# All engines in the order of the program: background pieces, their evictions and small shares of vector and scalar work in a two-layer graph network

## The chip, the cores and the metric

The kernel runs on one core of a Trainium2 chip. Its time is the device time of one execution in microseconds (us). The engines are named as in the profile: PE is TensorE (PEld its weight loads), DVE is VectorE, ACT is ScalarE, POOL is GpSimd, SP is SyncE, which issues DMAs. PEclk is the clock that TensorE was granted, as a share of full speed. All data are 32-bit floats.

## The reference

Two residual layers over 16 graphs of 1024 nodes with 256 channels. The first weighs the adjacency matrix by how similar the nodes' channel means are, makes queries from it, and runs attention with four heads of 64. The second multiplies by a normalised adjacency, and has two linear maps, each with a batch norm over all 16 × 1024 rows.

```python
# layer 0; x is (16, 1024, 256)
h = jnp.maximum(_layernorm(x, axis=-1), 0.0)
fea = jnp.transpose(h, (0, 2, 1))
c_adj = jnp.mean(fea, axis=1)
diff = c_adj[:, None, :] - c_adj[:, :, None]
A = jnp.abs(jnp.abs(jax.nn.sigmoid(diff) - 0.5) - 0.5) * 2.0
A_s = (A + jnp.transpose(A, (0, 2, 1))) * 0.5
g = jax.nn.relu(jnp.einsum('bcn,bnm->bcm', fea, adj[None] * A_s) * para.reshape(1, C, N))
q = jnp.transpose(g, (0, 2, 1)).reshape(B, N, 4, 64).transpose(0, 2, 1, 3)
kv = (h @ kv_w).reshape(B, N, 2, 4, 64).transpose(2, 0, 3, 1, 4)
attn = jax.nn.softmax(jnp.einsum('bhnd,bhmd->bhnm', q, kv[0]) * scale, axis=-1)
x = x + jnp.einsum('bhnm,bhmd->bhnd', attn, kv[1]).transpose(0, 2, 1, 3).reshape(B, N, C)
# layer 1
h = jnp.maximum(_layernorm(x, axis=-1), 0.0)
A_norm = adj + jnp.eye(n)
deg = A_norm.sum(0) + A_norm.sum(1) - jnp.diagonal(A_norm)
A_hat = A_norm * rsqrt(deg)[:, None] * rsqrt(deg)[None, :]
agg = jnp.einsum('nm,bmd->bnd', A_hat, h).reshape(-1, d)
y = jax.nn.relu(_batchnorm(agg @ W1.T + b1, g1, be1))
x = x + _batchnorm(y @ W2.T + b2, g2, be2).reshape(b, n, -1)
```

## The kernel before

**Two parts.** `layers(False)` does the first layer and the second one up to the hidden values `y` (512 channels), which go to HBM (`y1_d`), as does x after the first layer (`x1_d`). The batch norm needs statistics over all graphs, so `second("f", flag)` starts when the last `y` is there: it loads `y` in 32 blocks, applies the norm and a relu on ACT (L707), multiplies by `w2` on PE (L717), and after a second batch norm (L738) transposes, adds x and stores the result (L750 to L757). This last stretch is called the tail. A `layers(True)` behind a condition does attention with a shift by the row maximum; it is not executed here.

**The attention loop** (`attention`, L583) sets the order. A graph has four units `(b, k, f)`: a pair of heads `k` and half of the nodes `f`. A unit has four steps, so a graph has 16 steps. On PE a step issues:

1. `scores` (L500): two score tiles, each then raised by an Exp on ACT (L508). Their PSUM pool has two buffers.
2. `finish` (L575), if a unit ended in the step before: four transposes of its output `os`, added to x on DVE (L579).
3. a TOP piece, if one is due: four transposes, either of broadcast channel means (`cbp`, L149) or of h (`htp`, L241).
4. `values` (L540): the product of the step before's Exp tiles with v.
5. `divide`, if that ended a unit: `sums` (L557), a product with ones of the accumulated Exp tiles `acc` (adds on DVE, L526 and L529). On DVE follow four reciprocals (L563), the product with `os` (L564), and two reductions that watch for overflow (L566, L567).
6. one to four background pieces from the generator `bg`.

**Background pieces.** `background(b)` yields, while graph b is in attention, the work of its neighbours in pieces of four or eight matmuls, each with an estimated cost in us (1.71): the queries of graph b+1 (`pg`, evicted by a multiply on DVE, L299, and a relu on ACT, L301), its keys and values (`pk`, L315 on ACT; `pv`, L332 on DVE), the aggregation of graph b-1 (`pa`, L368 on DVE), its hidden product (`py`, L386 on ACT, statistics on DVE, L387, store by POOL, L388), and the TOP pieces for graph b+2. As many pieces are issued in a step as `total`, spread over the 16 steps, makes due (L605). `weave` lets a side generator advance by one item with each piece.

Pieces share two PSUM banks:

```python
        def bank(name):
            return ps_mm.tile([P, FB], F32, tag="mm", name=name)
```

A piece that opens a bank waits until the second last user of the banks has been evicted.

**Vector and scalar work beside it.** `weights` (L247) makes the weighted adjacency of a query piece: a load of adj, two Abs (L261) and a Tanh (L268) on ACT, a product on DVE (L269), all in a pool of four buffers. `norm_relu` (L194) is a layer norm with relu: statistics on DVE (L211, L212), a reciprocal root on POOL (`rsqrt`, L76), relus on ACT (L218). `degrees` and `graph` (L161, L177) make the normalised adjacency once, in graph 0, in eight tiles that use the same four buffers as the adj tiles.

**What sets the order.** PE issues in the order of the program; DVE, ACT, POOL and SP are put in order by a scheduler:

```python
                with tc.manual_schedule(engines={mybir.EngineType.PE}):
                    run(norm_relu(0, True), differences(0), transposed(0))
                    weights(0, 2)
                    run(keys_values(0))
```

`second` stands outside of it, and all its engines are put in order by the scheduler.

Of the kernel before, what the change touches and what calls it, by code (L numbers as in the profile page):

```python
# [23 lines left out]
def gnn_two_layers_kernel(  # L24
# [38 lines left out]
    stats1 = const.tile([P, HC, B * NH, 6], F32, name="stats1")  # L63
    stats2 = const.tile([P, CC, B * NH, 6], F32, name="stats2")
# [16 lines left out]
    def layers(shifted):  # L81
# [20 lines left out]
        csums, cbcs, weighted = {}, {}, {}  # L102
        complete = set()

# [31 lines left out]
        nc.sync.dma_start(out=para_sb, in_=para.rearrange("(k p) n -> p k n", p=P))  # L136
# [3 lines left out]
        def broadcast_row(dst, col, name):  # L140

            for g in range(NT // 4):
                cb = p2.tile([P, 4, P], F32, tag="cb", name=f"cb_{name}_{g}")
                nc.vector.tensor_copy(
                    cb, col[:, 4 * g : 4 * g + 4].unsqueeze(2).to_broadcast([P, 4, P])
                )
                pt = bank(f"cbp_{name}_{g}")
                for j in range(4):
                    nc.tensor.transpose(pt[:, j * P : (j + 1) * P], cb[:, j, :], ident)  # L149
                nc.scalar.copy(dst[:, g * FB : (g + 1) * FB], pt)  # L150
                yield 0.5
# [9 lines left out]
        def degrees():  # L161
# [3 lines left out]
            for t in range(NT):  # L165
                a = load_adj_t(t, "at1")
                db = p2.tile([P, P], F32, tag="cb", name=f"db_{t}")
                nc.vector.tensor_mul(db, a[:, t * P : (t + 1) * P], ident)
                nc.vector.tensor_reduce(diag[:, t : t + 1], db, AX.X, ALU.add)
                nc.vector.tensor_reduce(col[:, t : t + 1], a, AX.X, ALU.add)  # L170
                yield 0.0
# [3 lines left out]
            yield 0.0  # L175

        def graph():  # L177

            dbc = p1.tile([P, N], F32, tag="cbc", name="dbc")
            yield from broadcast_row(dbc, dinv, "deg")  # L180
            for t in range(NT):
                a = load_adj_t(t, "at2")
# [11 lines left out]
        def norm_relu(b, first):  # L194


            tag = "a" if first else "b"
            src = xs[b]
            st6 = p2.tile([P, NT, 6], F32, tag="st6", name=f"st6_{tag}_{b}")
            mv = p2.tile([P, NT, 2], F32, tag="mv", name=f"mv_{tag}_{b}")  # L200
            sm = p2.tile([P, 3, NT], F32, tag="lnsm", name=f"lnsm_{tag}_{b}")
            if first:
                csums[b] = p2.tile([P, NT], F32, tag="csum", name=f"csum_{b}")
            h = p2.tile([P, NT, C], F32, tag="h", name=f"h_{tag}_{b}")
            hs[tag, b] = h
            for half in range(2):
                ts = range(half * NT // 2, (half + 1) * NT // 2)
                sl = slice(ts[0], ts[-1] + 1)
                rstd, shift, tmp = (sm[:, i, sl] for i in range(3))
                for t in ts:  # L210
                    nc.vector.bn_stats(st6[:, t, :], src[:, t, :])  # L211
                    nc.vector.bn_aggr(mv[:, t, :], st6[:, t, :])  # L212
                rsqrt(rstd, mv[:, sl, 1], EPS, tmp)
                nc.vector.scalar_tensor_tensor(
                    shift, mv[:, sl, 0], -1.0, rstd, op0=ALU.mult, op1=ALU.mult
                )
                for t in ts:
                    nc.scalar.activation(  # L218
                        h[:, t, :],
                        src[:, t, :],  # L220
                        AF.Relu,
                        bias=sm[:, 1, t : t + 1],
                        scale=sm[:, 0, t : t + 1],
                        accum_out=csums[b][:, t : t + 1] if first else None,
                    )
                yield 0.0

        TOP = -1.0

        def transposed(b):  # L230

            h = hs["a", b]
            hts[b] = []
            for k in range(CC):
                ht = p3.tile([P, N], F32, tag="ht", name=f"ht_{b}_{k}")
                hts[b].append(ht)
                for g in range(NH):
                    pt = bank(f"htp_{b}_{k}_{g}")
                    for j in range(FB // P):
                        t = g * (FB // P) + j  # L240
                        nc.tensor.transpose(  # L241
                            pt[:, j * P : (j + 1) * P], h[:, t, k * P : (k + 1) * P], ident
                        )
                    nc.vector.tensor_copy(ht[:, g * FB : (g + 1) * FB], pt)
                    yield 0.5

        def weights(b, upto):  # L247

            csum, cbc = csums[b], cbcs[b]
            made = weighted.setdefault(b, [])  # L250
            while len(made) <= min(upto, NH * NP - 1):

                q, th = divmod(len(made), NP)
                a = load_adj(q, th, f"adj_{b}_{q}_{th}")
                w = p4.tile([P, TH, FB], F32, tag="w", name=f"w_{b}_{q}_{th}")
                if b == 0:
                    nc.vector.tensor_reduce(
                        rows[:, q, th * TH : (th + 1) * TH], a, AX.X, ALU.add
                    )
                for t in range(TH):  # L260
                    nc.scalar.activation(  # L261
                        w[:, t, :],
                        cbc[:, q * FB : (q + 1) * FB],
                        AF.Abs,
                        bias=csum[:, th * TH + t : th * TH + t + 1],
                        scale=-1.0,
                    )
                nc.scalar.activation(w, w, AF.Tanh, scale=-0.5 / C)  # L268
                nc.vector.scalar_tensor_tensor(w, w, 1.0, a, op0=ALU.add, op1=ALU.mult)  # L269
                made.append(w)  # L270

        def differences(b):

            cbcs[b] = p1.tile([P, N], F32, tag="cbc", name=f"cbc_{b}")
            yield from broadcast_row(cbcs[b], csums[b], f"c{b}")

        def queries(b):
# [3 lines left out]
            for q in range(NH):  # L281
                cols = slice(q * FB, (q + 1) * FB)
                pgs = [bank(f"pg_{b}_{q}_{k}") for k in range(CC)]
                for th in range(NP):
                    i = q * NP + th
                    weights(b, i + 3)
                    for k in range(CC):
# [9 lines left out]
                        if th == NP - 1:  # L297
# [3 lines left out]
                            nc.scalar.activation(dst, dst, AF.Relu, scale=SCALE)  # L301
# [35 lines left out]
        def aggregate(b):  # L337

            h = hs["b", b]
# [8 lines left out]

            ats[b] = []
            for g in range(NH):  # L350
# [3 lines left out]
                for th in range(NP):  # L354
                    i = g * NP + th
                    load(i + 2)
# [14 lines left out]
        def hidden(b):  # L371
# [6 lines left out]
            for g, j in parts:  # L378
# [8 lines left out]
                nc.vector.bn_stats(stats1[:, j, i, :], y)  # L387
                nc.gpsimd.dma_start(out=y1_d[i][:, j, :], in_=y)  # L388
                yield 1.71

        def normed(b):
            halves = norm_relu(b, False)
            for half in range(2):
                while (b, half) not in complete:
                    yield 0.1
                yield from halves if half else [next(halves)]
            nc.gpsimd.dma_start(out=x1_d[b], in_=xs[b])

        def load_and_norm(b):
            load_x(b)  # L400
            yield 0.0
            yield from norm_relu(b, True)

        def weave(main, *sides):

            side = (piece for part in sides for piece in part)
            for cost in main:
                yield cost + next(side, 0.0)
            yield from side

        def background(b):

            nothing = iter(())
            more = b + 1 < B
            if b == 0:
                yield from weave(queries(1), degrees())
                yield from weave(keys_values(1), graph())
                yield from load_and_norm(2)
            else:
                if more:  # L420
                    yield from weave(queries(b + 1), normed(b - 1))
                    yield from keys_values(b + 1)
                else:
                    yield from normed(b - 1)
                yield from weave(
                    aggregate(b - 1), load_and_norm(b + 2) if b + 2 < B else nothing
                )
            products = hidden(b - 1) if b > 0 else nothing
            if b > 0:
                yield next(products)  # L430
            if b + 2 < B:

                made = chain(differences(b + 2), transposed(b + 2))
                for i in range(3):
                    yield TOP
                    yield next(made) + next(made)
                    if i == 0:
                        weights(b + 2, 2)
                    yield from islice(products, 3)
            yield from products  # L440

        def run(*parts):
            for part in parts:
                for _ in part:
                    pass
# [66 lines left out]
        class Unit:  # L512


            def __init__(self, b, k, f):
                self.at = (b, k, f)
                self.name = f"{b}_{k}_{f}"
                self.acc = None

# [31 lines left out]
            def divide(self):  # L551
# [8 lines left out]
                inv = p1.tile([P, FB], F32, tag="inv", name=f"inv_{self.name}")  # L560
                for j in range(FB // P):
                    c = slice(j * P, (j + 1) * P)
                    nc.vector.reciprocal(inv[:, c], self.pt[:, c])  # L563
                nc.vector.tensor_mul(self.os, self.os, inv)  # L564
# [252 lines left out]
```

## Time and profile before

| | us |
|---|---|
| median of 3 runs | 2894.21 |
| lowest, highest | 2893.5, 2896.43 |
| profiled execution, its own time | 2898.18 |
| its span in the trace | 2896.4 |
| PE busy in the span | 2733.5 (94%) |
| DVE busy | 1606.6 (55%) |
| ACT busy | 1257.2 (43%) |
| POOL busy | 189.6 (7%) |

The mean granted clock is 0.983. The span runs from the first recorded instruction to the last; the execution's own time is 1.8 us longer. Busy times are sums over the span; a matmul's end is modelled, so that records of one engine can overlap slightly. A line of a timeline has the start, the duration (of a run of like instructions), the engine, line and operation, the tile written and the tiles read, and in brackets the idle time before it and what ended it. In the list of waits a row has the engine, what waited, what it waited for, and then the sum in us, the number of times and the longest. Attention of graph 0 starts at 68.7 us in the trace, that of graph 1 at 199.8, and the neighbours after that about 158 us apart; the second part starts at 2590.3 and the tail at 2812.

### The profile page before, as it was taken

To read this page: it belongs to the slowest core of one execution; us is meant where nothing else is said; L and a number is where in the kernel's file an instruction comes from. 1 tells how busy PE (TensorE), PEld (TensorE's weight loads), DVE (VectorE), ACT (ScalarE), POOL (GpSimd) and SP (SyncE) were. 2 spreads that over 40 slices of the span, in tenths; PEclk is the share of its full clock that TensorE was granted. 3 is DMA by queue.
4 is the path that set the end of the run, shared out by engine and by line. 5 is a ranking of instruction groups with operands and counts; after the bars stand their busy time and mean duration, and the time that the engine had idled before them with its cause. 6 is when DMAs were issued, how large, how long until landed. Compare 5 with 4: busy or idle time off the path is not lost. (4 is left out here: it accounts for less than half of the span.)

```text
span 2896.4 us, 31623 instructions
## 1 busy us (share of the span) xinstructions
PE 2733.5 (94%) x12426; PEld 999.9 (35%) x12426; DVE 1606.6 (55%) x2407; ACT 1257.2 (43%) x1795; POOL 189.6 (7%) x318
## 2 busy tenths in 40 slices
PE   7989999999999999999999999999999999989994
PEld 3233333333333333333333333333333333334443
DVE  5775555646465655555464656555554645624444
ACT  5554444425363444444253634444443524324434
POOL 1010000001010000000010100000000001000001
PEclk9999999999999999999999999999999999999997
DMA  4341312213131313122131313131222212145449
GB/s 162 115 154 58 108 60 95 80 62 113 44 124 37 107 51 105 58 95 80 62 113 44 124 37 113 42 108 59 96 79 62 98 46 79 64 184 188 145 145 349
DMA packets 99182, 285.80 MB, mean 99 GB/s; under 512 B 8656, under 2 KB 25552, under 8 KB 90832
## 3 DMA queue, kind: packets, MB, share of 16 engines
q1 hardware_dynamic: 80848, 212.37, 22.4%
q0 software_dynamic: 18176, 71.31, 6.4%
q8 instruction: 100, 1.64, 0.2%
q14 instruction: 58, 0.48, 0.1%
HBM read 212.35 MB, written 71.30 MB: 98 GB/s over the span
## 5 line engine op out<-in xcount | busy, mean ns | idle before, releaser
L508 ACT ACTIVATE p<-sc 128x1024 f32<-128x1024 f32 x512 | 498.3, 1018 | 831.2 <-PE sc L500 831.1
L529 DVE TENSOR_TENSOR acc<-acc,p 128x1024 f32<-128x1024 f32 x384 | 468.8, 1221 | 353.9 <-ACT p L508 343.7
L500 PE MATMUL sc<-q,k 64*128 64x512 f32 x2048 | 514.8, 621 | 1.4 <-ACT p L508 1.4
L112 PE MATMUL pg<-w,h_a 128*64 128x512 f32 x2048 | 466.7, 604 | 42.8 <-DVE q L299 42.7
L540 PE MATMUL o<-p,v 128*64 128x512 f32 x2048 | 499.9, 609 | 0.0
L112 PE MATMUL pa<-aht,h_b 128*64 128x512 f32 x2048 | 456.4, 592 | 0.0
L500 PEld LDWEIGHTS sc<-q,k 64*128 64x128 f32 x2048 | 178.6, 189 | 329.5 <-issue 310.2
L112 PEld LDWEIGHTS pg<-w,h_a 128*64 128x64 f32 x2048 | 148.7, 138 | 341.3 <-issue 283.6
L112 PE MATMUL py<-at,w 128*64 128x512 f32 x1024 | 234.0, 596 | 28.0 <-ACT y L386 20.7
L112 PEld LDWEIGHTS pa<-aht,h_b 128*64 128x64 f32 x2048 | 147.0, 137 | 287.0 <-issue 280.9
L717 PE MATMUL pz_f<-yin_f,w 128*128 128x512 f32 x512 | 222.1, 596 | 11.3 <-ACT yin_f L707 11.3
L563 DVE RECIPROCAL inv<-sums 128x128 f32<-128x128 f32 x256 | 217.1, 910 | 25.1 <-PE sums L557 25.1
L540 PEld LDWEIGHTS o<-p,v 128*64 128x64 f32 x2048 | 125.0, 137 | 297.4 <-issue 296.5
L526 DVE TENSOR_TENSOR acc<-p,p 128x1024 f32<-128x1024 f32 x64 | 78.4, 1225 | 241.9 <-ACT p L508 241.9
L269 DVE SCALAR_TENSOR_TENSOR w<-w,adj 128x1024 f32<-128x1024 f32 x128 | 154.6, 1217 | 100.2 <-ACT w L268 73.6
L261 ACT ACTIVATE w<-cbc,csum 128x512 f32<-128x512 f32 x256 | 171.7, 715 | 70.1 <-PE pg L112 70.0
L388 POOL DMA_DIRECT2D y_d<-y x128 | 71.9, 562 | 1520.8 <-ACT y L386 1516.8
L386 ACT ACTIVATE y<-py,vec 128x512 f32<-128x512 f32 x128 | 87.5, 684 | 192.0 <-PE py L112 190.5
L707 ACT ACTIVATE yin_f<-yin_f,sm 128x512 f32<-128x512 f32 x128 | 93.6, 802 | 126.4 <-DMA yin_f<-y_d 126.4
L717 PEld LDWEIGHTS pz_f<-yin_f,w 128*128 128x128 f32 x512 | 97.9, 192 | 134.8 <-issue 124.7
L268 ACT ACTIVATE w<-w 128x1024 f32<-128x1024 f32 x128 | 134.4, 1050 | 1.0
L112 PEld LDWEIGHTS py<-at,w 128*64 128x64 f32 x1024 | 69.8, 137 | 175.9 <-issue 121.3
(86 smaller groups left out, 1904.4 us busy)
## 6 DMA issues: line engine op xcount, KB each, us to landing
adj<-in_adj_dram SPq DMA_DIRECT2D x128, 512.0 KB, 4.1
aht<-aht_d SPq DMA_DIRECT2D x128, 512.0 KB, 3.3
y_d<-y POOLq DMA_DIRECT2D x128, 256.0 KB, 3.9
yin_f<-y_d SPq DMA_DIRECT2D x32, 1024.0 KB, 4.8
x<-in_x_dram SPq DMA_DIRECT2D x32, 512.0 KB, 4.8
x_d<-x POOLq DMA_DIRECT2D x16, 1024.0 KB, 4.2
xo_f<-x_d SPq DMA_DIRECT2D x16, 1024.0 KB, 9.5
out_dram<-xo_f POOLq DMA_DIRECT2D x16, 1024.0 KB, 20.3
```

What stands on the lines that cost most here:

```text
L112: nc.tensor.matmul(dst[r], left[:, r], right, start=start, stop=stop)
L261: nc.scalar.activation(w[:, t, :], cbc[:, q * FB : (q + 1) * FB], AF.Abs, bias=csum[:, th * TH + t : th * TH + t + 1], scale=-1.0,)
L268: nc.scalar.activation(w, w, AF.Tanh, scale=-0.5 / C)
L269: nc.vector.scalar_tensor_tensor(w, w, 1.0, a, op0=ALU.add, op1=ALU.mult)
L386: nc.scalar.activation(y, py, AF.Identity, bias=b1[:, j : j + 1])
L500: nc.tensor.matmul(sc[:, e, :], ks[b][k][r, m * P : (m + 1) * P], qs[b][k][r, f * FB : (f + 1) * FB], start=True, stop=True,)
L508: nc.scalar.activation(pr, sc, AF.Exp)
L529: nc.vector.tensor_add(self.acc, self.acc, pr)
L540: nc.tensor.matmul(self.o[r, :], vs[b][k][:, m, r], pr[:, e, :], start=(m == 0), stop=(m == NT - 1),)
L563: nc.vector.reciprocal(inv[:, c], self.pt[:, c])
L707: nc.scalar.activation(y[:, j, :], y[:, j, :], AF.Relu, bias=sh1[:, j : j + 1], scale=s1[:, j : j + 1],)
L717: nc.tensor.matmul(pz, w2[:, j, k * P : (k + 1) * P], y[:, j, :], start=(j == 0), stop=(j == HC - 1),)
```

## The change

All of `layers(False)` and `second` runs in the order of the program, on every engine. So the program's order now also says where each eviction and each piece of vector and scalar work stands.

- Evictions are issued with their piece; work that reads an eviction's result (the relu of queries, the statistics of y) is put in a queue by `soon` and issued by `advance` after the next piece.
- `norm_relu`, `weights` and `degrees` become generators that give up a small share at a time (`Norm`, `weigh`, `degrees`), and `weave` takes one share of each side behind each piece.
- A unit's end is split: two reciprocals behind the first piece, two and the product behind the next ones or at the end of the pieces, the two watch reductions at the end of the following step. The adds of a step are issued right behind its scores.
- The TOP pieces are three whole ones (the `cb` copies come a piece earlier) with up to three `py` pieces and three shares of weights between. Graph 1's are moved into graph 0's attention, and most of graph 14's hidden products into that of graph 15 (`endings`). The totals follow.
- `x` of graph b+3 is loaded at the end of `normed(b)`, aht tiles one further ahead, and `para` later.
- At the boundary the first batch norm's scale is made in two halves of two channel blocks each, and the first two blocks of y are worked off half by half. The aggregation of the statistics (L678) is done where the last `y` are made.

The diff, cut to its core:

```diff
+        def soon(action):
+            queue.append(action)
+        def advance(pieces):
+            due = queue[:]
+            queue.clear()
+            cost = next(pieces, None)
+            for action in due:
+                action()
+            return cost
+        def weave(main, *sides):
+            for i, cost in enumerate(main):
+                for start, side in sides:
+                    if i >= start:
+                        cost += next(side, 0.0)
+                yield cost
...
             for t in range(NT):
                 a = load_adj_t(t, "at1")
-                db = p2.tile([P, P], F32, tag="cb", name=f"db_{t}")
+                yield 0.0
+                db = p2.tile([P, P], F32, tag="db", name=f"db_{t}")
...
+        def weigh(b):
+            load()
+            for slot in range(2 * NH * NP + 1):
+                i, odd = divmod(slot, 2)
+                if not odd and i < NH * NP:
+                    if i + 1 < NH * NP:
+                        load()
...
+                    for t in range(TH):
+                        nc.scalar.activation(
...
+                            AF.Abs,
...
+                if odd:
+                    nc.scalar.activation(made[i], made[i], AF.Tanh, scale=-0.5 / C)
+                if not odd and i > 0:
+                    w, a = made[i - 1], adjs[i - 1]
+                    nc.vector.scalar_tensor_tensor(w, w, 1.0, a, op0=ALU.add, op1=ALU.mult)
...
+                yield 0.0
+        AHEAD = 6
...
                             nc.vector.tensor_mul(dst, pgs[k], para_sb[:, k, cols])
-                            nc.scalar.activation(dst, dst, AF.Relu, scale=SCALE)
+                            soon(
+                                lambda dst=dst: nc.scalar.activation(
+                                    dst, dst, AF.Relu, scale=SCALE
+                                )
+                            )
...
                 nc.scalar.activation(y, py, AF.Identity, bias=b1[:, j : j + 1])
-                nc.vector.bn_stats(stats1[:, j, i, :], y)
                 nc.gpsimd.dma_start(out=y1_d[i][:, j, :], in_=y)
+                def stats(y=y, i=i, j=j):
+                    nc.vector.bn_stats(stats1[:, j, i, :], y)
...
+                soon(stats)
                 yield 1.71
...
+        def prepare(b, products):
+            cbs = columns_of(csums[b], f"c{b}")
+            yield from islice(products, 1)
+            yield TOP
+            differences(b, cbs)
+            yield 1.0
+            w = weighers[b]
+            for k in range(CC):
+                yield from weave(islice(products, 3), (0, islice(w, 3)))
+                yield TOP
+                transposed(b, k)
+                yield 1.0
+            yield from products
...
         def background(b):
...
+                yield from prepare(1, nothing)
+                yield from weave(queries(1), (0, weighers[1]), (0, degrees()))
...
+            before = hidden(b - 1)
+            gather = aggregate(b - 1)
+            if b + 1 < B:
+                yield from weave(queries(b + 1), (0, weighers[b + 1]))
+                yield next(gather)
+                yield from weave(keys_values(b + 1), (0, normed(b - 1)))
             else:
+                yield from weave(endings.pop(), (2, normed(b - 1)))
+                yield next(gather)
             if b + 2 < B:
+                yield from weave(gather, (7, Norm(b + 2, True).all()))
+                yield from prepare(b + 2, before)
+            elif b + 2 == B:
+                yield from gather
+                endings.append(before)
+            else:
+                yield from gather
+                yield from weave(before, (0, normed_last()))
...
-                inv = p1.tile([P, FB], F32, tag="inv", name=f"inv_{self.name}")
-                for j in range(FB // P):
-                    c = slice(j * P, (j + 1) * P)
-                    nc.vector.reciprocal(inv[:, c], self.pt[:, c])
-                nc.vector.tensor_mul(self.os, self.os, inv)
...
+                self.later = [lambda: invert(0), lambda: invert(1), scale]
+                self.watch = watch
+            def behind_piece(self):
+                if self.later:
+                    self.later.pop(0)()
+            def behind_pieces(self):
+                while self.later:
+                    self.behind_piece()
...
-                        total = 41.0 * (b + 1 < B) + 41.0 * (b > 0) + 6.0 * (b + 2 < B)
-                        total -= 12.0 * (b == B - 1)
+                        total = 41.0 * (b + 1 < B) + 27.3 * (b > 0) + 6.0 * (b + 2 < B)
+                        total += 13.7 * (0 < b < B - 2) + 27.4 * (b == B - 1) + 3.0 * (b == 0)
+                        total -= 10.3 * (b == B - 1)
                     made = scores(*unit.at, g)
-                    adds = list(made)
+                    for pr in made:
+                        unit.add(pr)
...
                 while done < due and not top:
-                    cost = next(bg, None)
-                    if adds:
-                        unit.add(adds.pop(0))
+                    cost = advance(bg)
                     if cost is None:
                         break
                     if cost == TOP:
                         top = True
-                    else:
-                        done += cost
-                for pr in adds:
-                    unit.add(pr)
+                        break
+                    done += cost
+                    if ended is not None and cost > 1.0:
+                        ended.behind_piece()
+                if ended is not None:
+                    ended.behind_pieces()
+                if finished is not None:
+                    finished.watch()
...
-                with tc.manual_schedule(engines={mybir.EngineType.PE}):
-                    run(norm_relu(0, True), differences(0), transposed(0))
...
+                run(norm.all())
+                differences(0, columns_of(csums[0], "c0"))
+                for k in range(CC):
+                    transposed(0, k)
+                run(weave(keys_values(0), (8 - AHEAD, islice(weighers[0], AHEAD))))
+                nc.sync.dma_start(out=para_sb, in_=para.rearrange("(k p) n -> p k n", p=P))
+                load_x(1)
+                run(weave(queries(0), (0, weighers[0]), (5, Norm(1, True).all())))
+                attention()
+                run(aggregate(B - 1), hidden(B - 1))
...
+            for half in range(2):
+                for i in range(2):
+                    relu(i, half)
+                for i in range(2):
+                    for k in range(CC):
+                        product(i, k, half)
+                        if half == 1:
+                            keep(i, k)
...
-    layers(False)
-    second("f", flag)
+    with tc.manual_schedule():
+        layers(False)
+        second("f", flag)
```

## The prediction

> **What bounds the kernel now.** I read first the busy time of each engine (columns: busy us, share of the span, instructions), then two rows of the forty slices of the span.
>
> ```profile
> PE 2733.5 (94%) x12426; PEld 999.9 (35%) x12426; DVE 1606.6 (55%) x2407; ACT 1257.2 (43%) x1795; POOL 189.6 (7%) x318
> ...
> PE   7989999999999999999999999999999999989994
> PEclk9999999999999999999999999999999999999997
> ```
>
> TensorE is the bound: 2733.5 of 2896.4 us, nine tenths or more in nearly every slice. VectorE and ScalarE have room (55%, 43%). A change of order that leaves TensorE's work alone can at most give back its idle time, 163 us, and what the clock loses. So the second view is what TensorE waited for (us in total, times, longest):
>
> ```profile
> PE pg L112 <- DVE q L299: 42.7, 14, 3.3
> PE py L112 <- ACT y L386: 20.7, 14, 1.6
> PE ot L575 <- DVE os L564: 17.9, 7, 8.0
> ...
> PE pz_f L717 <- ACT yin_f L707: 11.3, 1, 11.3
> ...
> PE py L112 <- DVE ht L244: 7.3, 13, 0.6
> ```
>
> Three rows come once a graph: pg 3.2, py 1.57 and py 0.56, 5.3 us in each of some 13 graphs, 70.7 in all. Third, TensorE's timeline in such a graph (start, duration, idle before and who ended it):
>
> ```profile
> 548.87 3.19 PE L112 MATMUL pg<-w,h_a 128*64 128x512 f32 x8 [3.19 <-DVE q L299]
> ...
> 657.70 1.94 PE L112 MATMUL py<-at,w 128*64 128x512 f32 x8 [1.57 <-ACT y L386]
> ...
> 708.42 1.94 PE L112 MATMUL pg<-w,h_a 128*64 128x512 f32 x8 [3.19 <-DVE q L299]
> ```
>
> The same eight matmuls after the same 3.19 of idling take 3.19 in one graph and 1.94 in the next. The scores behind the slow ones take 2.38 instead of 1.99, so an idle time of that length costs about 1.65 us more every other graph (starts of neighbouring graphs are 157.91 and 159.56 apart). Elsewhere 3.05, 3.12 and 3.34 were followed by slow matmuls, 1.57, 1.51 and 1.29 were not; 2.57 near the end was.
>
> Last, VectorE around the end of a unit, since its order is what changes:
>
> ```profile
> 644.07 3.39 DVE L563 RECIPROCAL inv<-sums 128x128 f32<-128x128 f32 x4 [0.39 <-PE sums L557]
> 647.38 0.63 DVE L368 COPY at<-pa 128x512 f32<-128x512 f32 x1
> 647.93 0.68 DVE L564 TENSOR_TENSOR os<-os,inv 128x512 f32<-128x512 f32 x1
> ```
>
> The scheduler lets the reciprocals run at once, and os is ready at 648.6, before the transposes that read it (649.3).
>
> [...]
>
> **The change part by part.** Matmuls keep their number and size. Spacings used, all from timelines of the kernel before: background piece 1.72, score pair 1.92, values 1.77, sums 0.86, four transposes 0.5 to 0.6, add or weight product 1.13, a reciprocal 0.83, 512-wide copy, product or statistics 0.60, cb copy 0.33, TensorE to its consumer 0.21.
>
> *Start.* The first half is normalised by itself and no row reduction stands between transposes; the first k product moves from 20.91 to about 18.0. Row reductions among the v copies give back some 0.5: **−2.4**.
>
> *First graph* (64.3 to 199.8, 135.5 us; idle stretches 3.12, 3.05, 7.97 and 3.26). The degree tiles now sit in VectorE's queue between evictions. Their loads need one of four buffers that weight tiles release late; reciprocals stand behind them. Walking the new order I find waits of 1.8, 7.0, 1.3, 5.9 and 4.3 us in place of the old ones: 137.5, **+2**, with −10 to +10 as bounds, since the arrival of those loads decides (3.6 to 4.3 us each when alone).
>
> *Graphs 1 to 13, what goes.* The multiply of a pg bank is issued right behind its piece, and the next two pieces are one of another bank and one spare: 3.2 goes, with its slow rate. The y evictions no longer stand behind two Abs and a Tanh (0.62 + 0.62 + 0.94), so 1.57 and 0.56 go in their present form. Removed: 5.32 idle + 0.82 (half of 1.65) = 6.14.
>
> *What comes.* In the step that ends the unit whose background is the last aggregate piece, VectorE has, with the step's first score at 0: two adds, the at copy that waits for that piece (6.47 to 7.07), two reciprocals (8.73), two cb copies (9.4), two reciprocals (11.06), one statistics (11.66), the os product (12.34). The ot transposes are wanted at 1.92 + 1.77 + 0.86 + 2 × 1.72 + 1.92 ≈ 10.0: TensorE waits **2.45**. Queued behind it on VectorE are the next adds and the ht copies. In the following TOP steps a py bank waits for the ht copy that stands behind a weight product (itself behind Tanh, behind y evictions), two statistics, the two watch reductions and two adds: free at 19.5, wanted at 17.6, **1.9**; and again 30.5 against 29.5, **1.0**. Sum 5.35. If one in five is followed by the slow rate, 0.33 more: 5.68. Bounds: nothing (if I mis-order by one share each time) to 5.35 + 2 × 1.65 = 8.65. Taken: 5.68 − 6.14 = −0.46 a graph, × 13 = **−6**. The watch reductions (2 × 0.60) move to the next step; they are free except in the 1.9 above. On SP the load of x for graph b+3 now waits for the store of x1 (4.2 to land) with later aht loads behind it; three aht tiles are issued ahead of it and the k and v pieces, 16 × 1.72, lie between. On POOL the rsqrt pair of a norm now keeps its place among the y stores (0.56 each), but norms and hidden products fall into different parts of a graph. No TensorE wait in the view is for these loads or for POOL, so I count 0; with the cover gone a load would cost about 4 us a graph.
>
> *Graph 14* loses its 1.06 wait: **−1**. *Graph 15* has idle waits of 3.34, three of 0.75, 0.56, 1.29, 0.33 = 7.8, and about 1.5 of slow rate, because it runs out of background work; eight pieces more of it are moved in from graph 14. I leave 2 us: **−7**.
>
> *Boundary.* The first pz waits 11.3:
>
> ```profile
> 2590.28 16.24 PE L717 MATMUL pz_f<-yin_f,w 128*128 128x512 f32 x33 [11.32 <-ACT yin_f L707]
> ...
> 2589.37 2.93 ACT L707 ACTIVATE yin_f<-yin_f,sm 128x512 f32<-128x512 f32 x4 [9.68 <-DMA yin_f<-y_d]
> ```
>
> ScalarE waited for the load of y, which waits for the last y store (issued 2579.99, landed 3.9 later, load issued 2584.31). The affine values were there at 2585.5. Halving the affine and the first blocks shortens work that is already covered: **0**; at best half the four relus, 1.5; at worst 1.5 lost by half sums in more banks. *Second stage* keeps its loads ahead and its single matmul order, *tail* 2812 to 2896 moves 314 GB/s with its DMA engines 84% busy: **0**.
>
> Sum: −2.4 + 2 − 6 − 1 − 7 = −14.4. Profiled: 2898.18 (span 2896.4 + 1.8 around it) − 14.4 = 2883.8. That execution stands 4.0 above the median of the runs, 2894.21, so the median becomes about **2880**; by the bounds that lie within this case, 2864 to 2896.
>
> **Rivals.** *More is gained:* the ht waits do not come, as ScalarE, less crowded, makes Tanh earlier than I think; only 2.45 a graph stays. 13 × (6.14 − 2.45) = 48, with 8 to 10 elsewhere: about 2836. For it: ScalarE is busy 43%; against it: both adds now come before the ht copies on VectorE. *Slower:* the half rate. Two new waits of 2.45 and 1.9 us follow each other within 8 us in every graph; if each is followed by 1.65 of slow matmuls, a graph costs 8.65 instead of 6.14, 13 × 2.5 = +33, −8 elsewhere: about 2919. It decides from a loss s where 13 × (5.35 + s − 6.14) = 8.4, s = 1.44 us a graph. For it: 2.57 of idling was slow once; against it: none of 1.6 or less was. *First graph worse:* loads held by late buffers hold VectorE for longer, +10; a question of size within the first case. *It does not act:* the order is written into the program, and the instruction streams of the changed kernel show it on all engines, so only an effect near zero is left.
>
> **Numbers.** My own case 0.50 (faster 0.37, same 0.10, slower 0.03), more gained 0.20 (faster), slow rate 0.25 (same 0.04, slower 0.21), no effect or something unseen 0.05 (same 0.01, slower 0.04). About 0.2%, 5.8 us, is what a measurement of this kernel can tell from no change. That makes 0.57 faster, 0.15 same, 0.28 slower. The range leaves out the far halves of both rivals, about 0.1 each: 2842 to 2918.
>
> **What would show it.** In the profile after, the rows pg L299 and py L386 of TensorE's waits should be gone; an ot row for os with about 13 waits near 2.5 us and a py row for the ht copy with 1 to 2 us should stand instead. Starts of neighbouring graphs should be about 158.3 apart, evenly. Graph 15 should show under 3 us of idling, the boundary still about 11. I am wrong if pg still waits, if the intervals between graphs exceed 160, if the ot row is missing, or if the first graph moves by more than 10.

## The result, and the profile after

| | before | after |
|---|---|---|
| median, us | 2893.86 (4 runs) | 2912.56 (4 runs) |
| lowest, highest | 2892.88, 2896.43 | 2911.14, 2914.55 |
| profiled execution, its span | 2898.18, 2896.4 | 2911.14, 2909.3 |

The change makes the kernel slower: the ratio is 1.0064, with a 95% interval of 1.0046 to 1.0081. The forecast was 14 us faster; it became 18.7 slower. The two profiled executions differ by 13.0 only, since that of before lies 4.3 above its median and that of after 1.4 below.

The page after, its busy times and two rows of its forty slices, shows that TensorE bounds the kernel as it did:

```profile
PE 2739.9 (94%) x12426; PEld 1009.3 (35%) x12426; DVE 1618.5 (56%) x2410; ACT 1268.7 (44%) x1795; POOL 191.1 (7%) x320
...
PE   7889999999999999999999999999999999989994
PEclk9999999999999999999999999999999999999997
```

TensorE is busy for 6.4 us more with the same 12426 instructions: some of them ran slower. The list of its waits (total us, times, longest) has the rows that the prediction asked for:

```profile
PE ot L724 <- DVE os L701: 46.7, 21, 6.0
PE py L145 <- DVE ht L334: 41.4, 26, 2.0
...
PE pz_f L878 <- ACT yin_f L870: 11.9, 1, 11.9
...
PE good_f L958 <- DVE ext L957: 2.2, 1, 2.2
```

The rows of before, pg for q in 14 graphs and py for y in 14, are gone. In their place stand, in each of 13 graphs, ot for os once and py for ht twice. TensorE's timeline (start, duration, in brackets the idle time before) gives their sizes and what follows them:

```profile
489.92 0.63 PE L724 MATMUL ot<-ident,os 128*128 128x128 f32 x4 [2.35 <-DVE os L701]
490.39 1.73 PE L188 MATMUL cbp_c<-ident,cb_c 128*128 128x128 f32 x8
492.05 2.88 PE L672 MATMUL o<-p,v 128*64 128x512 f32 x8
...
506.87 7.07 PE L145 MATMUL py<-at,w 128*64 128x512 f32 x24 [1.99 <-DVE ht L334]
...
520.20 1.94 PE L145 MATMUL py<-at,w 128*64 128x512 f32 x8 [1.46 <-DVE ht L334]
...
668.04 5.37 PE L145 MATMUL py<-at,w 128*64 128x512 f32 x24 [1.99 <-DVE ht L334]
...
679.33 1.94 PE L145 MATMUL py<-at,w 128*64 128x512 f32 x8 [1.11 <-DVE ht L334]
```

The waits are 2.35, 1.99 and then 1.11 (1.46 to 1.49 in three graphs), in each of the 13. Behind the first, the values take 2.88, where eight such matmuls take 1.94 at full rate; behind the second, the same 24 matmuls take 7.07 in one graph and 5.37 in another. VectorE's timeline over the same stretch shows why both waits are there:

```profile
483.98 0.69 DVE L481 COPY at<-pa 128x512 f32<-128x512 f32 x1 [2.04 <-PE pa L145]
484.59 1.76 DVE L698 RECIPROCAL inv<-sums 128x128 f32<-128x128 f32 x2
486.27 0.69 DVE L177 COPY cb_c<-csum 128x512 f32<-128x512 f32 x2
486.88 1.76 DVE L698 RECIPROCAL inv<-sums 128x128 f32<-128x128 f32 x2
488.55 0.63 DVE L503 BATCH_NORM_STATS2 stats<-y 128x6 f32<-128x512 f32 x1
489.11 0.67 DVE L701 TENSOR_TENSOR os<-os,inv 128x512 f32<-128x512 f32 x1
...
503.67 2.54 DVE L661 TENSOR_TENSOR acc<-acc,p 128x1024 f32<-128x1024 f32 x2
506.13 1.28 DVE L334 COPY ht<-htp 128x512 f32<-128x512 f32 x2
```

VectorE idles for 2.04 us in front of the at copy, which waits for its piece, while the reciprocals behind it could run: sums, which they read, ended at 482.22 on TensorE (481.19 + 1.03), and the first of them starts at 484.59, behind the copy. So os is ready only at 489.8, and the transposes start right then. At 503.67 two adds, for which nobody waits yet, stand ahead of the copies that free a bank. That these two places are what makes the waits is argued here from the order; the first three experiments test it.

By stages of the two profiled executions, with milestones on TensorE (the first scores of a graph, L500 or L631, the first pz, the first pt):

| stretch | before | after | difference | forecast |
|---|---|---|---|---|
| start to the first scores of graph 1 | 199.82 | 201.43 | +1.6 | -0.4 |
| graphs 1 to 13 | 2067.13 | 2081.69 | +14.6 | -6 |
| graphs 14 and 15, last products, boundary | 323.33 | 317.21 | -6.1 | -8 |
| second part up to the tail | 227.82 | 230.52 | +2.7 | 0 |
| tail | 78.3 | 78.45 | +0.2 | 0 |

The loss lies in graphs 1 to 13.

### The profile page after: what moved, and what is told of

Read it like the earlier page. It is cut to its first block, busy times and chain, and to the rows that moved or that the text cites. A ratio compares the mean times of both kernels' runs of the same rounds, so it can differ in the third digit from the quotient of the medians.

```text
span 2909.3 us, 31551 instructions
## 1 busy us (share of the span) xinstructions
PE 2739.9 (94%) x12426; PEld 1009.3 (35%) x12426; DVE 1618.5 (56%) x2410; ACT 1268.7 (44%) x1795; POOL 191.1 (7%) x320
## 5 line engine op out<-in xcount | busy, mean ns | idle before, releaser
L631 PE MATMUL sc<-q,k 64*128 64x512 f32 x2048 | 508.8, 615 | 0.5 <-ACT p L639 0.5
L672 PE MATMUL o<-p,v 128*64 128x512 f32 x2048 | 506.4, 616 | 0.0
L145 PE MATMUL pg<-w,h_a 128*64 128x512 f32 x2048 | 453.5, 592 | 3.0 <-DVE ht L334 2.0
L145 PE MATMUL py<-at,w 128*64 128x512 f32 x1024 | 248.6, 631 | 41.4 <-DVE ht L334 41.4
L631 PEld LDWEIGHTS sc<-q,k 64*128 64x128 f32 x2048 | 176.1, 186 | 320.8 <-issue 289.4
L503 DVE BATCH_NORM_STATS2 stats<-y 128x6 f32<-128x512 f32 x128 | 85.2, 681 | 95.7 <-ACT y L499 95.0
```

What stands on the lines that cost most here:

```text
L145: nc.tensor.matmul(dst[r], left[:, r], right, start=start, stop=stop)
L631: nc.tensor.matmul(sc[:, e, :], ks[b][k][r, m * P : (m + 1) * P], qs[b][k][r, f * FB : (f + 1) * FB], start=True, stop=True,)
L672: nc.tensor.matmul(self.o[r, :], vs[b][k][:, m, r], pr[:, e, :], start=(m == 0), stop=(m == NT - 1),)
```

## The experiments

All are timed against the kernel before on the same chip, and edits are to the changed kernel unless said otherwise. The changed kernel's 2912.56 is from the first comparison; since the medians of the kernel before lie between 2893.86 and 2895.9 in all of them, differences to it are good to some 2 us. A period is the time between the first transposes of a unit (ot) in one graph and in the next; the mean period is taken over the 12 from graph 1 to graph 13. Theory A was: the loss is the new waits, and the slow rate of TensorE after most of them. The rivals are given with each run.

**One wait at a time.** The first run takes two reciprocals out from behind the at copy (the second pair and the product then move up by one piece as well), and the second takes the adds out from in front of the ht copies; the third does both.

```diff
                     if g_last == NG - 1:
                         last.divide()
                         ended = last
+                        ended.behind_piece()
```

> The first two reciprocals of a unit stand right behind its sums, ahead of the next piece's eviction; nothing else moves. Theory A (the time lost is the two new idle stretches of each graph, and a slow stretch of TensorE after most of them): the ot wait of 2.35 falls to below 0.3 in all 13 graphs, the slow transposes and values behind it (1.65 in 8 graphs of 12) go, the py waits of 1.99 and 1.11 stay with their slow stretch. A graph's period falls from 160.06 to about 156.6, the time to about 2868. Theory B (a wait that is removed comes back at the next bank, because VectorE is late by the same amount): the ot wait falls, but the py waits grow by 1 to 2, and the time stays above 2895.

Measured: 2858.33 (ratio to before 0.987, 0.9852 to 0.9888), 54 below the changed kernel, more than the 44 expected. Its waits:

```profile
PE py L145 <- DVE ht L334: 40.1, 26, 2.0
...
PE ot L724 <- DVE os L701: 8.9, 3, 4.2
```

The 13 ot waits of the inner graphs are gone (three are left, in graph 0), the py waits did not grow. Theory B falls for this wait. The mean period is 156.68; in the changed kernel it is 1920.73 / 12 = 160.06.

```diff
-                    for pr in made:
-                        unit.add(pr)
+                    if not top:
+                        for pr in made:
+                            unit.add(pr)
...
                 if top:
                     done += advance(bg)
+                    if s < len(steps):
+                        for pr in made:
+                            unit.add(pr)
                     top = False
```

> In a step with a TOP piece the two adds stand behind it, so that the copies of the transposed h are ahead of them on VectorE. Theory A: both py waits (1.99 and 1.11 to 1.49) fall below 0.3, with the 1.70 that the 24 matmuls behind the first one lose in 10 graphs of 13; the ot wait stays. Period 160.06 to about 155.4, time about 2852. Theory B: the adds are late instead, Exp waits for its buffers and the scores for Exp; a wait of sc for p of 1 us or more stands in each graph, time above 2895.

Measured: 2839.09 (0.9805, 0.9788 to 0.9822), 73 below, 13 more than expected. No row of py is left in its waits, and no wait of sc for p of more than 0.4; ot stays:

```profile
PE ot L724 <- DVE os L701: 47.1, 21, 6.0
```

Periods are 154.09 in most graphs and 155.74 in those where a slow stretch follows the ot wait, 4 of 13; in the changed kernel it followed 9 of the same 13 waits, which is most of the surplus.

> Both edits. Theory A: no wait above 0.5 is left between graphs 1 and 13, period 152.2 to 152.6, time about 2810, below the kernel before by some 84. Theory B: less than the sum of the two gains, time above 2880.

Measured: 2795.76 (0.966, 0.9641 to 0.9679), 117 below the changed kernel, 14 more than expected, and 100 below the kernel before on that chip (2895.9). Busy times of a stretch of 80 us (columns: window, length, then busy us of PE, PEld, DVE, ACT and POOL, the clock, the DMA share and GB/s), first of after, then of this run:

```profile
640.00:720.00 80.00, 74.55 (x340) 26.32 (x336) 47.59 (x55) 41.96 (x54) 4.43 (x8) 0.98 0.24 81
```

```profile
640.00:720.00 80.00, 80.00 (x392) 28.59 (x388) 50.66 (x71) 41.52 (x55) 5.29 (x9) 1.00 0.19 66
```

In graphs 1 to 13 TensorE has no idle time of more than 0.15 us: every period is 151.88 or 151.89. The two single gains add up to 128; slow stretches fall differently in each run, so they need not add. The unit's end on VectorE now reads

```profile
469.12 1.77 DVE L698 RECIPROCAL inv<-sums 128x128 f32<-128x128 f32 x2 [0.33 <-PE sums L689]
470.84 0.69 DVE L481 COPY at<-pa 128x512 f32<-128x512 f32 x1
471.44 1.76 DVE L698 RECIPROCAL inv<-sums 128x128 f32<-128x128 f32 x2
473.12 0.69 DVE L177 COPY cb_c<-csum 128x512 f32<-128x512 f32 x2
473.73 0.68 DVE L701 TENSOR_TENSOR os<-os,inv 128x512 f32<-128x512 f32 x1
```

with the reciprocals in the time in which VectorE had waited. A graph lost 160.06 - 151.88 = 8.18 to waits: 5.45 to 5.8 idle, the rest the slow rate.

**Does the slow stretch come from the idling?** Matmuls on constant data ahead of the py waits keep TensorE busy without ending a wait sooner.

```diff
             for k in range(CC):
+                if k == 1 and b > 2:
+                    warm(4)
                 yield from weave(islice(products, 3), (0, islice(w, 3)))
                 yield TOP
                 transposed(b, k)
                 yield 1.0
+            if b > 2:
+                warm(2)
             yield from products
```

`warm(n)` issues n times `product(pt, ident, para_sb[:, 0, :FB], True, True)` into the PSUM tile of sums and ot.

> Eight and four matmuls of 128*64 x 512 on constant data are issued just ahead of the two waiting py pieces, into a bank that nothing reads: they fill 1.72 of the 1.99 and 0.86 of the 1.11 to 1.49, and end no wait sooner. It adds work and leaves the result as it is. If the slow stretch behind py comes from the idling (theory A), the 24 matmuls behind it take 5.37 in every graph instead of 7.07 in most, the period falls by about 1.3 and the time by 15 to 20, to about 2894. If the slow stretch has another cause (the mix of transposes and matmuls, or chance; theory C), 7.07 stays and the time is 2912 or a little more.

Measured: 2918.18 (1.0083, 1.0063 to 1.0102), where 2894 was expected. The fill was twice as long as meant: it took 3.43 and 1.72 us, some 2.05 more in each graph than the waits that it fills, so the time decides nothing. The trace has no wait of py left, and a slow stretch behind py in none of the 13 graphs; 9 still follow an ot wait. With the size halved (`warm(2)`, `warm(1)`):

> As the run that keeps TensorE busy, with the fill in the size of the idling: 1.72 ahead of the first waiting py piece, 0.86 ahead of the second (the run before had twice as much by a wrong count of matmul records). Adds work, leaves the result as it is. Theory A (idling brings the slow stretch): idle 0.27 and 0.25 to 0.6 are left before py, never a slow stretch behind it, period 157.4 with 1.65 more in the graphs whose ot wait is followed by one, on average about 158.2; time about 2889. Theory C (slow for another reason): period 160, time 2912.

Measured: 2887.95 (0.9982, 0.9974 to 0.9989), as expected, and 25 below the changed kernel, though it does more work. Its py waits:

```profile
PE py L145 <- DVE ht L334: 7.8, 26, 0.6
```

All these periods lie between 157.62 and 159.64; those with an extra 1.65 are the ones with a slow stretch behind the ot wait (4 of 13). Behind py there is none. Theory C falls: without the idling the slow stretch does not come.

**Length or place?** In the run with the reciprocals first, one and the same wait of 1.98 was followed by the slow stretch in ten graphs of 13, and these were the last ten in a row, at a period of 157.10. In the traces before and after, all changes of the granted clock (33 and 53) are whole multiples of 3.413 us apart, to within 0.01: a fixed grid, whose stretches are called windows below. Two more runs shift the place, with four and eight matmuls on constant data (0.86 and 1.72 us; `range(1)`, then `range(2)`) in step 2 of each graph; the edit of the first run is in both:

```diff
+                if s % per_graph == 2 and 0 < b < B - 2 and s < len(steps):
+                    pt = ps_t.tile([P, FB], F32, tag="t", name=f"extra_{s}")
+                    for i in range(1):
+                        product(pt, ident, para_sb[:, 0, :FB], True, True)
                 while done < due and not top:
```

> The kernel with the reciprocals first (only the py waits of 1.98 and 1.11 left, the first one followed by a slow stretch in 9 graphs of 12, the last 9 in a row), plus four matmuls (0.86) on constant data per graph, far from the waits; it adds work and leaves the result as it is. Theory W (the throttle looks at fixed stretches of about 3.41 us, and an idle time counts only where it lies well inside one; the period of 157.1 is 46.03 of them, so that graph after graph meets the same place): with 0.86 more the place moves on by 2.66 or 0.95 from graph to graph, and about half of the graphs, 5 to 7 of 12, are slow. Theory L (the length of the idling decides, with some chance): 9 of 12 stay slow.

Measured in a single execution: 2863.72; slow in 5 graphs of 13, mostly every other one. The mean period is 156.98, 0.30 above the run without the added 0.86.

> The same with eight matmuls (1.72) per graph. Theory W: after a graph without slow stretch the place moves by 0.11, after one with it by 1.81, out of the slow zone of about 1.3: the place comes to rest outside, and at most 3 graphs of 12 are slow; the period is 157.1 in most, no longer than without the added work. Theory L: 9 of 12 slow, mean period 158.4.

Measured in a single execution: 2865.79; slow in 1 graph of 13. All other periods are 157.12 to 157.14, the mean is 157.27, only 0.59 above the run without the added 1.72. TensorE's timeline, first of the run with the reciprocals first, then of this one:

```profile
806.80 7.07 PE L145 MATMUL py<-at,w 128*64 128x512 f32 x24 [1.98 <-DVE ht L334]
...
963.92 7.07 PE L145 MATMUL py<-at,w 128*64 128x512 f32 x24 [1.98 <-DVE ht L334]
```

```profile
498.19 5.37 PE L145 MATMUL py<-at,w 128*64 128x512 f32 x24 [1.98 <-DVE ht L334]
...
655.32 5.37 PE L145 MATMUL py<-at,w 128*64 128x512 f32 x24 [1.98 <-DVE ht L334]
```

The idle time is the same 1.98 in all four lines. Theory L falls: which graphs are slow follows from where the wait falls in the grid. 46 times 3.413 is 157.0, and a kernel whose period is 157.10 meets almost the same place in each graph. Behind the waits of the changed kernel's graphs 1 to 13 each slow stretch is one window at half clock, 19 in all. Two waits of 1.98 us in the run with the reciprocals first, cut along the grid (columns: window, length, busy us of PE, clock, DMA share and GB/s):

```profile
647.72:651.13 3.41, 1.70 (x8) 1.00 0.45 165
651.13:654.54 3.41, 3.15 (x16) 1.00 0.00 0
804.73:808.14 3.41, 1.43 (x8) 1.00 0.06 23
808.14:811.55 3.41, 3.41 (x11) 0.50 0.07 28
```

The first wait, which ends at 651.39, is cut by the edge at 651.13: 1.71 of idling lie in one window and 0.26 in the next, and the clock stays. The second, which ends at 806.80, lies in one window with all of its 1.98, and the next window runs at half clock. The other waits of that run agree: cut along the same grid, the first three of the 13 have 1.91, 1.87 and 1.71 in one window, and the 24 matmuls behind them take 5.37; the other ten, which start 0.09 to 0.90 behind an edge, have all of their 1.98 in one window, and the matmuls take 7.07. (The width of the slow zone in the expectation, about 1.3, was the author's estimate; these places leave 0.81 to 1.61 for it.) So it is the idle time within one window that counts here. In the traces before and after, 1470 windows at full clock lie between TensorE's first matmul and the second part: 1427 have less than 1.95 us of idling, and the half clock follows none of them; 26 have more than 2.02, and it follows each; of the 17 in between it follows 10. About 2 us of idling within one window were enough here.

**The written order against the scheduler.** The changed program, but with only TensorE in its order:

```diff
-    with tc.manual_schedule():
+    with tc.manual_schedule(engines={mybir.EngineType.PE}):
         layers(False)
-        second("f", flag)
+    second("f", flag)
```

> The changed program, but only TensorE in its order; VectorE, ScalarE, GpSimd and SyncE are ordered by the scheduler, as in the kernel before. If the written order of VectorE is what makes the two waits, the ot wait goes (the scheduler lets reciprocals run when sums are there), the py waits for ht shrink below 1, and the time is below 2880. If the waits come from the order of the pieces on TensorE, they stay, near 2912.

Measured: 2832.18 (0.9784, 0.9768 to 0.98), 80 below the changed kernel and 62 below the kernel before. Its inner graphs are 155.04 apart, none is slow, the ot waits there have shrunk to 0.28 and the py waits to 0.87, and the largest row of its inner waits is

```profile
PE pg L145 <- DVE q L406: 22.1, 13, 1.8
```

So the changed program without its written order on the other engines is a gain of 62, and that order costs 80. The other way round, in the kernel before, with the first part in the program's order on every engine:

```diff
-                with tc.manual_schedule(engines={mybir.EngineType.PE}):
+                with tc.manual_schedule():
```

> The kernel before with one edit: the first layer's part runs in the order of the program on all engines, not on TensorE alone (the second part stays with the scheduler). If a written order as such costs time where the program wasn't laid out for it, VectorE's product with weights waits for Tanh with evictions behind it, and norms come in blocks of eight operations: waits of 2 us and more several times a graph, most with a slow stretch, 2960 to 3100. If the written order as such is harmless and only the changed program's places of reciprocals and adds are at fault, it is 2880 to 2930.

Measured: 3097.66 (1.0703, 1.0683 to 1.0722).

```profile
PE pg L112 <- DVE q L299: 129.1, 15, 12.0
PE cbp_c L149 <- DVE cb_c L144: 68.2, 18, 13.3
```

The old program in a written order costs 203. The first of the two expectations held: a written order needs a program that is laid out for it. Which part of the changed layout does this, the small shares or the places of the evictions, is not shown.

**A version that beats both.** To the two edits come two more: degree tiles get a second share between load and use, and the vector part of the overflow check is issued two blocks of y before its matmul (how `flag` is split for this is left out below).

```diff
                 a = load_adj_t(t, "at1")
                 yield 0.0
+                yield 0.0
...
+                if i == B * NH // 2 - 2 and midway is not None:
+                    midway(None)
                 if i == B * NH // 2 and midway is not None:
```

> Both edits (reciprocals first, adds behind a TOP piece) and two more: the degree tiles are used two pieces after their load is issued, not one, so that VectorE waits less for them in graph 0; the vector part of the overflow check is issued two blocks of y ahead of its matmul. The ot waits of 4.3 and 4.2 in graph 0 fall by half or more (-4 to -6), the wait of 2.2 for the check goes: 2796 to about 2788. If the loads of the degree tiles are bound by their buffers, not by their use, graph 0 stays and it is 2793.

Measured: 2790.15 (0.9639, 0.9626 to 0.9652), 5.6 below the run with both edits, on another chip. The wait for the check is gone, and the stretch from the first pz to the first pt falls from 231.66 to 228.65. In graph 0 the first ot wait falls from 4.34 to 1.20, and a new one of 1.55 for cb_deg comes; the later ot wait of 4.15 stays (4.58), against what was expected. It falls where the normalised tiles are made, which the edit leaves alone.

## Why the prediction was wrong

**The places and sizes of the waits were right.** Forecast were an ot wait of 2.45 and py waits of 1.9 and 1.0 in each inner graph; measured are 2.35, 1.99 and 1.11 (1.46 to 1.49 in three graphs). The pg and y waits went. Walking the written order of VectorE with durations from the profile before was good to 0.1 us for the first two waits, and to 0.5 for the third. (For the first, the prediction's own terms add up to 9.91 and 12.34, which gives 2.43.) The idle time of graphs 1 to 13 grows by 2.7 only, from 69.25 to 71.93.

**The step that failed is "if one in five is followed by the slow rate, 0.33 more".** Of the 13 ot waits 9, and of the 13 first py waits 10 were followed by it, at 1.65 to 1.7 us each; none of the third waits was. That is about 2.4 us a graph instead of 0.33. The prediction had put its turning point at 1.44 and the case in which each of the two waits is slowed at 2919; the measured 2912.56 lies between that point and that case, so the second rival came true in part. Graphs 1 to 13 add up as follows: the record of the clock has 64.8 us at half rate after and 30.7 before, and half of that time is lost (1.70 in one window of 3.41 behind the py wait, 7.07 - 5.37), which makes 17.1 more; idling is 2.7 more; measured is +14.6, and some 5 us of work at full rate that went are not put down to anything.

The prediction gives no reason for "one in five". Its evidence was of lengths: 3.19 was slowed every other time, 1.57 never, 2.57 once. In the run with the reciprocals first, waits of one length, 1.98, were slowed where all of it lay in one window and not where 1.91 or less did: the place of the wait counts. The prediction had the clue in hand: the intervals of before mostly alternate between 157.91 and 159.56, which add up to 317.47, or 93.0 times 3.413; for much of the trace the wait of 3.19 met the same two places again and again. "Every other time" was no chance to be scaled down, but a pattern of that one period, and no count could be carried over to a new one. The fair entry was a range, from 5.45 with no slow stretch to 8.8 with two. For a place at random, an estimate from the figures above puts the chance that at least 1.98 us of a wait lie within one window of 3.41 at (3.41 + 2.35 - 2 × 1.98) / 3.41 = 0.53 for the ot wait and 0.42 for the first py wait. That is 1.57 us a graph, already past the turning point. That 19 of 26 came, and not about 12, was the luck of these periods.

**Graphs 14 and 15** were to give 8 with the boundary and gave 6.1. In graph 14 a wait of 0.72 stands where 1.06 had been. In graph 15, without the boundary, the idle time falls from 7.8 to 3.3 (waits of ot of twice 0.37, 1.44 and 1.11), where 2 was forecast, and the slow stretch behind the 3.34 is gone. These terms were right in kind and a little too large.

**Start and first graph** together: forecast -0.4, measured +1.6, within the bounds. The waits in graph 0 were foreseen at 1.8, 7.0, 1.3, 5.9 and 4.3; measured are 1.95, 4.72, 1.44, 6.03 and 4.17, and one of 1.14 that was not foreseen. **Boundary:** forecast 0, with 11 us of waiting for the load; measured 11.85 for 11.32. ScalarE still waits for the load of y there; that the halves bring nothing is read from this, and no run without them was made. **Second part:** forecast 0, measured +2.7. The missed step is a wait of 2.2 of TensorE for the vector part of the overflow check (good L958), whose matmul is now held to its place; the last experiment takes it away. **Tail:** unchanged, as forecast. Of the prediction's own signs of being wrong one came: the intervals between graphs exceed 160 in 7 of 13, up to 161.31, where 158.3, evenly, was foreseen.

## What to carry to other kernels

A written order is worth it only if each engine's queue is walked: what can run already must stand ahead of what waits (the reciprocals above stood behind a copy that waited for 2.04 us), and what nobody waits for must stand behind what frees a bank. Here two edits that do this are worth 117 us, and the order without them costs 80 against the scheduler. Here a wait of 1.98 us on TensorE, the bounding engine, cost its length or 1.7 us more, by how much of it lay within one window of 3.413 us in the clock's grid. Do not price such a wait by its length alone. In a periodic kernel the place can repeat from graph to graph (here the slow stretch came 10 times in a row, every other time, or once in 13), so enter the case with the slow rate and the case without, and remove the wait.

## What the runs showed of the hardware

- A wait of 1.98 us was followed by about 1.7 us lost in 10 of 13 graphs (reciprocals first), in 5 of 13 (0.86 us of work added) or in 1 of 13 (1.72 added), by where it fell. Adding 1.72 us of work to each graph cost 0.59 us in the mean, since it removed slow stretches.
- In the traces before and after the granted clock changes only on a grid of 3.413 us. Less than 1.95 us of idling in one window at full clock was never followed by half clock in the next (1427 windows), more than 2.02 always (26). In between, at 1.98 to 2.01, both occur (10 of 17 followed); the traces do not show what decides there (the ends of matmuls are modelled, which may blur the figure).
- In the run under the scheduler a wait of 1.69 to 1.76 us stood in 13 graphs at places all over the grid, and was never followed by a slow stretch, even where all of it lay in one window (columns as above; idle 1.69 in the first):

```profile
380.75:384.17 3.42, 1.73 (x10) 1.00 0.81 249
384.17:387.58 3.41, 3.41 (x16) 1.00 0.57 198
```

- One slow window cost much the same behind each of three waits: 1.70 us behind 1.98, 1.65 behind 2.35 and behind 3.19, close to half of 3.413. One wait of 3.19 in the kernel before was followed by two windows at half clock, and the interval grew by 2.75.
